# Order of loads, stores and the last division around the turned tile in a fused transformer layer

## The chip, the cores and the metric

The kernel runs on one core of a Trainium2 chip. The metric is the device time of one execution in microseconds, as the median of several runs. A profile of one execution was taken by the hardware profiler. The core's engines are TensorE (PE, with its weight loads as PEld), VectorE (DVE), ScalarE (ACT), GpSimd (POOL) and SyncE (SP, here the queue that issues most DMAs); each runs its instructions in the order of the program and waits for the others by semaphores.

## The reference

The input x has the shape (2, 256, 128, 128): batch, time T, bands FB, channels C. All is float32. Three residual steps follow one another:

```python
xt = _ln(x, ln_t_w, ln_t_b).transpose(0, 2, 1, 3)
x = x + _mha(xt, t_wi, t_bi, t_wo, t_bo, H_T, cm).transpose(0, 2, 1, 3)   # over time, causal
xf = _ln(x, ln_f_w, ln_f_b)
x = x + _mha(xf, f_wi, f_bi, f_wo, f_bo, H_F, bm)                          # over bands, |i - j| <= 16
xn = _ln(x, ln_n_w, ln_n_b)
h = jax.nn.gelu(xn @ w1.T + b1, approximate=False)                         # 128 -> 512
x = x + (h @ w2.T + b2)                                                    # 512 -> 128
```

Both attentions have 4 heads of 32 channels.

## The kernel before

The work is cut into 384 groups of 512 tokens, each kept as 128 partitions by 4 tiles by 128 channels. The first 128 groups are attention over time (class `OverTime`); they write their result to DRAM. Then come 16 runs of 16 groups: eight groups of attention over bands (`OverBands`) and, on the same tokens, eight groups of the feed-forward layer (`FeedForward`). A run of groups is called a run below, its band groups B0 to B7 and its feed-forward groups F0 to F7.

Every group passes the same stations. `load` brings x from DRAM (for band groups one DMA of 256 KB, `x<-x` in the profile). `statistics` and `root` make mean and variance (`stats`, `mv`, VectorE) and the inverse root (`rstd`, GpSimd). `normalize` makes `xh` and `turn` a transposed tile `z`, both on VectorE; `turn` also issues four DMAs from z to a DRAM tile `turned`. `fetch` issues one DMA that brings the turned tile back as `xnT`, channels on partitions, which is what TensorE needs. A band group then makes queries and keys (`bank<-xnT,wf`), values, scores (`qT,kT`), exponentials `pf`, their sums (`pf,ones`) and weighted values (`pf,v`); `divide` divides by the sums on VectorE and yields `oT`; `output` multiplies by the output weights (`wn,oT`); `finish` adds the residual on VectorE (`x<-bank,x`). A feed-forward group makes the hidden layer (`bank<-xnT,w1f`, 16 products for every one of its two halves), the gelu on ScalarE (`hT`), the second product (`w2T_sb,hT`) and the residual (`res`); `put` stores pairs of groups to `out`.

One loop over n, in `run`, issues pieces of about 18 groups at a time: it loads group n + 14, fetches n + 2, turns n + 3 (and in parts of a run n + 6), does the main products of n, and divides, outputs and finishes n - 1 and n - 2. The order in which the loop's body calls the pieces is the order of the instructions on each engine. `bands[i]` and `feeds[i]` tell whether group n - 2 + i is a band or a feed-forward group; `turn` is true in the one step per run where n is F0 and n - 1 is B7, so that the division in it is the last one of the run. That last division is exact (`invert_exactly`: RECIPROCAL to `ln`, then `u` and `oT`); the others start from ScalarE's logarithm and exponential (`r`).

In the profile all of these instructions have line 979, that of a helper that passes every instruction on, so that they are told apart by their tiles.

Of the kernel before, what the change touches and what calls it, by code (L numbers as in the profile page):

```python
# [691 lines left out]
class OverTime(Attention):  # L692
# [5 lines left out]
    early, late = (1, 2), (0, 3)  # L698
# [285 lines left out]
class BoundedPath:  # L984
# [364 lines left out]
    def run(self, x, out):  # L1349
        groups = list(self.groups(x, out))  # L1350

        def do(n, *names):
            if 0 <= n < len(groups):
                for name in names:
                    getattr(groups[n], name)()

        def at(n, kind):
            return 0 <= n < len(groups) and isinstance(groups[n], kind)

        def do_at(n, kind, *names):  # L1360
            if at(n, kind):
                do(n, *names)
# [13 lines left out]
        def at_turn(i):  # L1376
            return not 0 <= i < len(groups) or hasattr(groups[i], "turned")

        def turn_ahead(n):
            for i in (n + 3, n + 6):  # L1380
                ahead = at(n + 3, OverBands) and at(i, OverBands) and i not in run0
                if not at(i, OverTime) and (i == n + 3 or ahead) and not at_turn(i):
                    do(i, "normalize", "turn")
# [8 lines left out]
        for n in range(len(groups) + 2):  # L1392
            feeds = [at(n - 2 + i, FeedForward) for i in range(5)]
            bands = [at(n - 2 + i, OverBands) for i in range(5)]
            turn = feeds[2] and bands[1]
# [61 lines left out]
            do_at(n + 2, (OverBands, FeedForward), "fetch")  # L1457

            self.storing = self.scalar if feeds[2] and n < len(groups) - NT else self.sync
            do_at(n - 2, FeedForward, "put")  # L1460
            if n == 3:
                k.late_rows()
            if n == 5:
                k.late_weights()
            for i in {0: (), 1: (), 2: (14, 15), 3: (16, 17)}.get(n, (n + 14,)):
                do(i, "load")
            turn_ahead(n)
            if n != 1:
                do_at(n + 4, OverTime, "normalize", "turn")
            if old is not None:  # L1470
                do(n - 2, "finish")
            if n == 0:
# [28 lines left out]
            if bands[1] and bands[2]:  # L1501
                groups[n - 1].keep = True
                groups[n - 2].keep_output = bands[3]
                groups[n - 1].divide(partial(do, n - 2, "finish"))
            else:
                do(n - 1, "divide")
            if n == 1:
                do(5, "normalize", "turn")
            if n == 2:
# [111 lines left out]
```

## Time and profile before

| | |
|---|---|
| median of 3 runs | 2633.51 us (2633.33 to 2635.23) |
| profiled execution: its own time, its span | 2635.07 us, 2633.3 us |
| TensorE, products busy | 2617.5 us (99%) |
| TensorE, weight loads busy | 1779.1 us (68%) |
| VectorE busy | 2136.7 us (81%) |
| GpSimd busy | 1960.3 us (74%) |
| ScalarE busy | 1820.1 us (69%) |
| granted TensorE clock | full speed over the whole span |
| DMA | 344.99 MB, mean 131 GB/s |

The span is the time from the first to the last instruction of the program; the execution's own time has the start and the end around it as well. Busy shares are averages over the first part (time, about 920 us) and the 16 runs. Products on TensorE overlap one another, and their ends are modelled, so what they wait is seen in the distances between their starts.

### The profile page before, as it was taken

The page shows a single profiled execution, that of the slowest core. Times are in us where ns is not written, and L with a number is a line of the kernel's source. Part 1 is how long each engine was busy: PE and PEld are TensorE (multiplying, and loading weights), DVE is VectorE, ACT ScalarE, POOL GpSimd, SP SyncE. Part 2 cuts the span into 40 slices and gives each one's busy share as a digit, 9 for nine tenths or more (in the row PEclk, how much of TensorE's full clock was granted, in tenths as well). Part 3 has the DMA queues.
Part 4 walks back from the last instruction along what each step waited for, and adds up shares of the span by engine and source line. Part 5 has one row for each costly group of instructions (what it writes and reads, how often), then busy time and mean ns, then how long its engine had stood idle before and what let it go on. Part 6 is the DMA issues. An engine that isn't in the chain of part 4 may idle for free.

```text
span 2633.3 us, 156638 instructions
## 1 busy us (share of the span) xinstructions
PE 2617.5 (99%) x68688; PEld 1779.1 (68%) x68688; DVE 2136.7 (81%) x6410; ACT 1820.1 (69%) x3543; POOL 1960.3 (74%) x2311
## 2 busy tenths in 40 slices
PE   9999999999999999999999999999999999999999
PEld 6666676667666666667666666666666676666665
DVE  8888888888888888878779788787787887977874
ACT  7889999998998875564655745646557466475563
POOL 7999999999999977766666666666676666657762
PEclk9999999999999999999999999999999999999999
DMA  6656556566565455445454454554544544545443
GB/s 156 164 148 158 148 152 155 150 154 156 144 156 150 122 131 139 105 117 131 106 142 116 117 133 107 131 131 107 142 109 118 133 110 124 132 105 141 106 102 88
DMA packets 469798, 344.99 MB, mean 131 GB/s; under 512 B 43120, under 2 KB 404464, under 8 KB 469104
## 3 DMA queue, kind: packets, MB, share of 16 engines
q1 hardware_dynamic: 418360, 310.28, 47.4%
q10 hardware_dynamic: 50744, 24.59, 3.4%
q8 instruction: 541, 8.86, 1.5%
q14 instruction: 153, 1.25, 0.2%
HBM read 167.98 MB, written 166.72 MB: 127 GB/s over the span
## 4 chain that ended last, share of the span: by engine, by line
PE 87%; DVE 9%; issue 1%; DMA 1%; POOL 1%; ACTq 0%; SPq 0%; ACT 0%; DVEq 0%; POOLq 0%
PE bank L979 87%; DVE xh L979 2%; DVE bank L979 1%; DVE ln L979 1%; DVE stats L979 1%; DVE u L979 1%; DVE x L979 1%; DVE oT L979 1%; POOL rstd L979 1%; DVE z L979 0%; DMA xnT<-turned 0%; DVE mv L979 0%; ACTq L979 0%; DMA turned<-z 0%; SPq L979 0%
## 5 line engine op out<-in xcount | busy, mean ns | idle before, releaser
L979 ACT ACTIVATE hT<-bank,b 128x512 f32<-128x512 f32 x512 | 342.1, 688 | 534.4 <-PE bank L979 368.8
L979 POOL TENSOR_SCALAR_AFFINE_SELECT pf<-pf 128x512 f32<-128x512 f32 x768 | 478.3, 637 | 244.0 <-ACT pf L979 217.6
L979 PEld LDWEIGHTS bank<-w2T_sb,hT 128*32 128x32 f32 x16384 | 466.2, 110 | 137.1 <-issue 109.2
L979 PE MATMUL bank<-xnT,wf 128*32 128x512 f32 x4096 | 511.5, 593 | 1.0 <-DVE xnT L979 0.5
L979 PE MATMUL bank<-w2T_sb,hT 128*32 128x128 f32 x16384 | 498.2, 273 | 0.8 <-issue 0.5
L979 PE MATMUL bank<-xnT,w1f 128*32 128x512 f32 x4096 | 497.9, 592 | 0.0
L979 ACT ACTIVATE p<-bank 128x512 f32<-128x512 f32 (+1 forms) x1024 | 430.7, 494 | 63.2 <-PE bank L979 62.9
L979 DVE TENSOR_SCALAR xh<-x,mv,rstd 128x160 f32<-128x160 f32 (+1 forms) x1012 | 392.4, 430 | 59.8 <-POOL rstd L979 49.4
L979 POOL TENSOR_SCALAR_AFFINE_SELECT p<-p 128x1024 f32<-128x1024 f32 (+2 forms) x384 | 365.0, 951 | 55.4 <-ACT p L979 47.1
L979 PEld LDWEIGHTS bank<-wf,xnT 128*32 128x32 f32 x8192 | 237.0, 110 | 151.5 <-issue 89.8
L979 POOL TENSOR_TENSOR p<-p,p 128x512 f32<-128x512 f32 x256 | 324.6, 1291 | 10.7
L979 DVE BATCH_NORM_STATS2 stats<-x 128x6 f32<-128x128 f32 x1536 | 328.9, 276 | 3.3 <-DMA x<-in_x 3.3
L979 DVE TENSOR_TENSOR bank<-bank,r 128x512 f32<-128x512 f32 x240 | 166.2, 693 | 194.0 <-ACT r L979 116.1
L979 PE MATMUL bank<-qT,kT 32*64 32x80 f32 (+4 forms) x16384 | 303.7, 271 | 3.0 <-issue 2.9
L979 PEld LDWEIGHTS bank<-qT,kT 32*64 32x64 f32 x16384 | 260.9, 131 | 55.0 <-ACT kT L979 50.7
L979 ACT ACTIVATE pf<-bank 128x512 f32<-128x512 f32 x512 | 264.4, 602 | 37.6 <-PE bank L979 37.5
L979 POOL TENSOR_SCALAR rstd<-mv 128x4 f32<-128x4 f32 x251 | 57.7, 230 | 304.8 <-DVE mv L979 304.1
L979 DVE STREAM_TRANSPOSE z<-xh 128x512 f32<-128x512 f32 x380 | 270.4, 711 | 15.2 <-DMA turned<-z 1.8
L979 PE MATMUL bank<-wn,oT 128*32 128x128 f32 x8192 | 278.3, 274 | 1.1 <-DVE oT L979 0.3
L979 POOL TENSOR_TENSOR rstd<-rstd,mhalf 128x4 f32<-128x4 f32 x251 | 260.8, 1039 | 20.9
L979 PE MATMUL bank<-wf,xnT 128*32 128x128 f32 x8192 | 272.8, 273 | 0.0
L979 PEld LDWEIGHTS bank<-wn,oT 128*32 128x32 f32 x8192 | 221.2, 110 | 25.6 <-DVE oT L979 12.6
(100 smaller groups left out, 3713.3 us busy)
## 6 DMA issues: line engine op xcount, KB each, us to landing
turned<-z SPq DMA_DIRECT2D x1520, 64.0 KB, 2.6
xnT<-turned SPq DMA_DIRECT2D x380, 256.0 KB, 3.4
x<-res SPq DMA_DIRECT2D x256, 128.0 KB, 2.5
x<-x SPq DMA_DIRECT2D x128, 256.0 KB, 4.6
x<-in_x SPq DMA_DIRECT2D x124, 256.0 KB, 4.4
out<-res ACTq DMA_DIRECT2D x184, 128.0 KB, 3.0
out<-res SPq DMA_DIRECT2D x68, 128.0 KB, 3.5
x<-in_x SPq DMA_DIRECT2D x4, 128.0 KB, 3.1
```

The costliest lines, as they stand in the source:

```text
L979: return self.tc.keep_in_program_order(emit(*args, **kwargs))
```

## The change

In a step that handles a band or feed-forward group (`ahead`), the load of group n + 14 is issued after `turn_ahead`, that is after the four DMAs of the turned tile; before, it was issued ahead of them. In the steps where n is a band group, the store of group n - 2 (`put`) is issued there too. In the one step of a run where `turn` is true, `turn_ahead` and what follows it now come after the division of B7; before, they came ahead of it. `turn_ahead` itself is unchanged.

```diff
             self.storing = self.scalar if feeds[2] and n < len(groups) - NT else self.sync
-            do_at(n - 2, FeedForward, "put")
+            if not bands[2]:
+                do_at(n - 2, FeedForward, "put")
...
-            for i in {0: (), 1: (), 2: (14, 15), 3: (16, 17)}.get(n, (n + 14,)):
-                do(i, "load")
-            turn_ahead(n)
+            def late(n=n, bands=bands):
+                if bands[2]:
+                    do_at(n - 2, FeedForward, "put")
+                do(n + 14, "load")
+
+            ahead = at(n, (OverBands, FeedForward))
+            if not ahead:
+                for i in {0: (), 1: (), 2: (14, 15), 3: (16, 17)}.get(n, (n + 14,)):
+                    do(i, "load")
+            if not turn:
+                turn_ahead(n)
             if n != 1:
                 do_at(n + 4, OverTime, "normalize", "turn")
+            if ahead and not turn:
+                late()
...
                 do(n - 1, "divide")
+            if turn:
+                turn_ahead(n)
+                late()
             if n == 1:
```

What this does to the order shows on two engines. On VectorE, at the end of the second run, before: `ln`, `u` and `oT` are the division of B7, `xh` and `z` belong to F3, the TENSOR_TENSOR on x is the `finish` of B6, and the last rows are the statistics of F4.

```order
L979 BN_STATS stats<-x_20822 128x6 x4
L979 BN_AGGR mv<-stats 128x2 x4
L979 TENSOR_SCALAR xh<-x_20822,mv,rstd 128x5x32 x4
L979 STREAM_TRANSPOSE z<-xh 128x512
L979 RECIPROCAL ln<-bank_112 128x512
L979 TENSOR_TENSOR x_21409<-bank_110,x_21409 128x512
L979 TENSOR_TENSOR u<-bank_114,ln 128x4x4x32
L979 TENSOR_SCALAR oT<-u 128x512
L979 BN_STATS stats<-x_21409 128x6 x4
```

And the same place after the change:

```order
L979 BN_STATS stats<-x_20834 128x6 x4
L979 BN_AGGR mv<-stats 128x2 x4
L979 RECIPROCAL ln<-bank_112 128x512
L979 TENSOR_TENSOR x_21421<-bank_110,x_21421 128x512
L979 TENSOR_TENSOR u<-bank_114,ln 128x4x4x32
L979 TENSOR_SCALAR oT<-u 128x512
L979 TENSOR_SCALAR xh<-x_20834,mv,rstd 128x5x32 x4
L979 STREAM_TRANSPOSE z<-xh 128x512
L979 BN_STATS stats<-x_21421 128x6 x4
```

The division and the residual addition within it have moved ahead of the normalization and the transposition of F3; this happens at all 16 ends of runs and is the only move on VectorE.

On SyncE, at the start of the second run, before (`out` is the store of the run before, `x` the load of a group of a later run):

```order
L979 DMA turned_22748<-z_22746 32x4x128 x4
L979 DMA xnT_22892<-turned_22301 128x512
L979 DMA out<-res_22249 32x8x128 x4
L979 DMA turned_22905<-z_22903 32x4x128 x4
L979 DMA xnT_23013<-turned_22438 128x512
L979 DMA x_23015<-x1_0_94 32x16x128
L979 DMA xnT_23138<-turned_22569 128x512
L979 DMA x_23015<-x1_0_94 32x16x128
L979 DMA xnT_23274<-turned_22748 128x512
L979 DMA x_23015<-x1_0_94 32x16x128
L979 DMA xnT_23410<-turned_22905 128x512
L979 DMA x_23015<-x1_0_94 32x16x128
```

And after, the same place and the rows that follow:

```order
L979 DMA turned_22901<-z_22899 32x4x128 x4
L979 DMA out<-res_22249 32x8x128 x4
L979 DMA xnT_23013<-turned_22438 128x512
L979 DMA x_23015<-x1_0_94 32x16x128
L979 DMA xnT_23138<-turned_22569 128x512
L979 DMA x_23015<-x1_0_94 32x16x128
L979 DMA xnT_23274<-turned_22748 128x512
L979 DMA x_23015<-x1_0_94 32x16x128
L979 DMA xnT_23410<-turned_22901 128x512
L979 DMA turned_23419<-z_23417 32x4x128 x4
L979 DMA x_23015<-x1_0_94 32x16x128
L979 DMA xnT_23558<-turned_23419 128x512
```

The stores (four DMAs, 15 times in the program) have gone behind the four turned DMAs, and so has each load that shares a step with a turned tile (78 loads), which puts the load between the turned DMAs and the fetch of that same turned tile. A load in a step without a turned tile stays where it was. TensorE, ScalarE and GpSimd keep their order.

## The prediction

> **What bounds the kernel now.** I read the page first: busy shares, then the chain that ended last (the queue's row has packets, MB and share of the DMA engines).
>
> ```profile
> span 2633.3 us, 156638 instructions
> PE 2617.5 (99%) x68688; PEld 1779.1 (68%) x68688; DVE 2136.7 (81%) x6410; ACT 1820.1 (69%) x3543; POOL 1960.3 (74%) x2311
> ...
> q8 instruction: 541, 8.86, 1.5%
> ...
> PE 87%; DVE 9%; issue 1%; DMA 1%; POOL 1%; ACTq 0%; SPq 0%; ACT 0%; DVEq 0%; POOLq 0%
> ```
>
> TensorE (PE) is busy for 99% of the span and carries 87% of the chain; the change takes no product away. So all that can be won is time in which PE's products start later than their steady pace. That is not read from busy time, since products overlap and their ends are modelled; it is read from starts. Next come the waits of PE and of its weight loads (PEld): engine, tile, releaser, then total us, times, longest.
>
> ```profile
> PEld bank L979 <- ACT hT L979: 21.6, 67, 0.4
> ...
> PEld bank L979 <- DVE oT L979: 12.9, 15, 1.1
> ...
> PE bank L979 <- issue: 5.4, 12, 1.3
> ```
>
> Two rows matter here: oT, the divided attention output that VectorE (DVE) makes, waited for 15 times, about once per run (there are 16); and "issue", where nothing that the program shows was waited for. The 12.9 us are idle time of the weight loads, which run ahead of the products, so they are a ceiling and not the loss. The loss I take from the timeline around the end of a run (start us, duration us, engine; the run whose last division starts at 1086.36):
>
> ```profile
> 1081.57 1.04 PE L979 MATMUL bank<-pf,ones 128*32 128x512 f32 x8
> 1082.24 0.36 DVE L979 BATCH_NORM_AGGREGATE mv<-stats 128x2 f32<-128x6 f32 x4
> 1084.08 1.61 DVE L979 TENSOR_SCALAR xh<-x,mv,rstd 128x160 f32<-128x160 f32 x4 [1.48 <-POOL rstd L979]
> 1084.17 1.90 PE L979 MATMUL bank<-xnT,w1f 128*32 128x512 f32 x16
> 1085.72 0.71 DVE L979 STREAM_TRANSPOSE z<-xh 128x512 f32<-128x512 f32 x1
> 1086.36 3.32 DVE L979 RECIPROCAL ln<-bank 128x512 f32<-128x512 f32 x1
> 1089.60 0.63 DVE L979 TENSOR_TENSOR x<-bank,x 128x512 f32<-128x512 f32 x1
> 1090.15 0.68 DVE L979 TENSOR_TENSOR u<-bank,ln 128x512 f32<-128x512 f32 x1
> 1090.24 1.04 PE L979 MATMUL bank<-xnT,w1f 128*32 128x512 f32 x8
> 1090.86 0.43 DVE L979 TENSOR_SCALAR oT<-u 128x512 f32<-128x512 f32 x1
> 1091.20 0.86 DVE L979 BATCH_NORM_STATS2 stats<-x 128x6 f32<-128x128 f32 x4
> 1091.34 1.08 PE L979 MATMUL bank<-wn,oT 128*32 128x128 f32 x32
> 1092.24 1.90 PE L979 MATMUL bank<-xnT,w1f 128*32 128x512 f32 x16
> ```
>
> VectorE idles 1.48 us for rstd, then normalizes (xh) and turns (z) a later group, and only then starts the division (RECIPROCAL, then u, then oT). The sums that the division needs were done at 1081.57 + 1.04 = 1082.61. PE's output product starts at 1091.34, the moment oT is there (1090.86 + 0.43 = 1091.29).
>
> **The change part by part.**
>
> *The last division of a run goes ahead of the normalization.* From the first hidden product of the run's second feed-forward group to that of its third, PE takes 1092.24 - 1084.17 = 8.07 us here. One run later PE arrives late for another reason, oT is already there, and the same stretch shows the pace without the wait:
>
> ```profile
> 1192.35 0.66 PE L979 MATMUL bank<-xnT,w1f 128*32 128x512 f32 x3
> ...
> 1200.15 0.66 PE L979 MATMUL bank<-xnT,w1f 128*32 128x512 f32 x3
> ```
>
> That is 7.80 us: the wait costs 0.27 us. I took this stretch for all 16 runs from PE's rows: two have 7.80 (this one and the twelfth), the others 8.02 to 8.18, so 0.22 to 0.38 each, 4.07 us over 14 runs. After the change the division starts when the sums are done: 1082.65 at the latest of its inputs. From RECIPROCAL to the end of oT takes 1091.29 - 1086.36 = 4.93 us, so oT ends at 1087.58, some 3.5 us before PE comes for it at 1091.07. All of the wait goes: -4.1 us. Bounds: 0 if something else is late at that place, -12.9 if all idle time of the weight loads counted; I take 4.1, since it is measured on PE's own starts.
>
> *What becomes late instead.* xh and z come behind oT. They take 1086.43 - 1084.08 = 2.35 us, so z ends at 1089.93 and not at 1086.43: 3.5 us later, at the 15 or 16 ends alike. z goes to DRAM (turned, four DMAs) and comes back as xnT; both are issued on SyncE's queue (SPq):
>
> ```profile
> 1085.27 0.44 SPq L979 DMA_DIRECT2D x<-x  x1
> 1086.46 1.75 SPq L979 DMA_DIRECT2D turned<-z  x4
> 1091.56 0.34 SPq L979 DMA_DIRECT2D xnT<-turned  x1
> 1091.93 0.43 SPq L979 DMA_DIRECT2D x<-x  x1
> ...
> 1098.31 1.90 PE L979 MATMUL bank<-xnT,w1f 128*32 128x512 f32 x16
> ...
> 2576.19 3.09 SPq L979 DMA_DIRECT2D turned<-z  x4
> 2580.65 0.34 SPq L979 DMA_DIRECT2D xnT<-turned  x1
> ...
> turned<-z SPq DMA_DIRECT2D x1520, 64.0 KB, 2.6
> xnT<-turned SPq DMA_DIRECT2D x380, 256.0 KB, 3.4
> ...
> x<-x SPq DMA_DIRECT2D x128, 256.0 KB, 4.6
> ```
>
> (The last three are issues: KB each, median us from issue to landing.) PE wants this xnT with the second eight of the 16 products at 1098.31, one step of 0.86 us later: 1099.17, and 0.27 earlier after the change, 1098.90. New path: z at 1089.93, four issues 1.75, then the wait for turned to land, then issue and landing of xnT, 3.4. The wait for turned is 1091.56 - 1088.21 = 3.35 us in this run and 2580.65 - 2579.28 = 1.37 in the last. With 1.37 xnT lands at 1096.5, 2.4 us early; with 3.35 at 1098.4, 0.5 early. So no wait at PE by the median landing; I count 0, and keep as its bound 1.6 us a run from the rival below. The statistics behind it start at 1089.93 and not at 1091.20, since the 1.48 us of waiting for rstd are now filled with division: the next group's z gains 1.3 us.
>
> *Loads issued behind the turned tile.* 78 loads x<-x, each 0.44 us of SPq, change places with a group's four turned DMAs. turned starts up to 0.5 us earlier and no longer has 256 KB just ahead of it; x comes up to 1.8 us plus the wait for z later. No product waits for either: x is loaded 14 groups ahead and first read by the residual's bias addition 8 groups ahead, six steps of some 7 us later (1099.17 - 1092.24 = 6.93 is one). Gain and loss on PE: 0. SPq itself waits for z more often with the load queued behind it, but what stands behind the load is the next xnT, which needs the same turned tile anyway. If that cover of some 40 us were gone, a load would cost its 4.6.
>
> *The last stores of a run behind the turned tile.* 15 times four stores out<-res, on SPq. What is fetched next there was turned several groups before, and stands behind both either way; the res buffer is written again a whole run later. 0.
>
> PE's order and its waits are otherwise the same instruction for instruction, so the sum is -4.1 us. Against the profiled execution: span 2633.3 - 4.1 = 2629.2, and with the 1.7 us that lie around its span (its own time is 2635.07) 2631.0. That execution stands 1.6 us above the median of the runs, 2633.51; against the median the sum is 2629.4.
>
> **The rivals.** A measurement of this kernel tells 0.2% (5.3 us) from no change, so faster begins below 2628.2 and slower above 2638.8.
>
> *Slower: the fetch of xnT queues behind the moved load.* The load used to be ahead of turned and is now between turned and the fetch of what was turned. If its 256 KB go ahead of xnT as a whole, xnT lands later by about what a load takes over a turned DMA, 4.6 - 2.6 = 2.0 us (my estimate from these medians). The margin of 0.5 to 2.4 us above then becomes a wait of up to 1.5 us; at 15 ends, 15 x 1.5 - 4.1 = +18 us, 2651.9 at worst, and with half of that per end +7.2 us, 2640.7, which is the value I give it. It decides from (5.3 + 4.1) / 15 = 0.63 us per end on. The Trainium skill, "DMA: Bandwidth & Descriptors", section on queues, rings and completion order, says that each DMA engine takes the descriptors of a ring in the order of the ring; by it the load's bytes do precede xnT's, and the sum would be this rival's. Against it: a load 0.4 us behind the fetch, as at 1091.93 in this run, already shares the engines with xnT in the median of 3.4 us, and the fetch is issued at least 1.4 us after the load, by when much of the load is under way. Chance 0.07.
>
> *Faster: PE's instruction pages come sooner as well.* The 12 waits named "issue" are in mid-product-group, like this one:
>
> ```profile
> 2325.58 0.74 PE L979 MATMUL bank<-qT,kT 32*64 32x80 f32 x39
> 2326.10 0.44 SPq L979 DMA_DIRECT2D x<-x  x1
> 2327.58 0.51 PE L979 MATMUL bank<-qT,kT 32*64 32x80 f32 x25 [1.25 <-issue]
> ```
>
> The instruction queue moved 541 packets of 8.86 MB / 541 = 16.4 KB, and PE's 2 x 68688 instructions make 254 per packet. The eleven such stalls over 0.45 us that I followed in the bands' and feeds' part all fall on the same place modulo 256 instructions, and each ends 1.3 to 1.7 us after a packet has ended. So PE waits there for its own next page of instructions, and the page comes over the DMA engines that the moved loads use. If the new places of the loads let the pages through, up to 5.4 us more go: 2629.4 - 5.4 = 2624.0, half of that 2626.7, the value I give it. It decides from 1.2 us on. For it: some of these stalls lie just behind a load, as this one. Against: others lie beside turned or out DMAs, which stay, the bytes are the same, and pages may as well come later. The Trainium skill, "Runtime: NRT & Kernel Launch", instruction fetch mechanics, has pages of 16 KiB fetched while the current one runs, at a cost that is mostly hidden; the page size agrees with the 16.4 KB, and by "hidden" this rival would be worth nothing, where the row shows 5.4 us. Chance 0.26.
>
> *Nothing: the wait is refilled.* At the ends of runs PE then waits for ScalarE's hidden layer or the late xnT, 0.27 us a run: 2633.5. For it: the weight loads wait for the hidden layer's hT 67 times already. Against: 0.4 us is the longest of these, all of them within idle time that the weight loads have anyway, and in the two runs with 7.80 us nothing of the kind took the wait's place. Chance 0.07.
>
> **How the numbers follow.** The forecast, 4.1 us off and pages within 1.1 us of now: 0.60, 2629.4, with a range of its own of 2628.3 to 2630.5. Same is the forecast and the refilled wait, 0.67; faster 0.26; slower 0.07. The range goes from 2625.5, past the middle of the faster rival, to 2634.0, past the refilled wait; what lies outside is the slower rival and the rest of the faster, under 0.2.
>
> **What would show it.** In the changed profile: the PEld wait for oT falls from 15 times to one or two; RECIPROCAL follows the aggregated statistics without the 1.48 us of idle time, and oT ends some 3.5 us before its product; the stretch of 8.07 us is 7.80 in all runs; z at the ends is 3.5 us later and the fetch of xnT lands still ahead of its product. The forecast is wrong if that product shows PE waiting for xnT, or if the "issue" waits change by more than 1.2 us.

## The result, and the profile after

The changed kernel took 2637.91 us (median of 22 runs, 2632.70 to 2647.36) where the kernel before took 2633.42 (22 runs, 2629.96 to 2639.59) beside it: 1.0018 times as long, 95% interval 1.0010 to 1.0027. That is about 4.5 us slower, where 4.1 us faster was forecast, and 3.9 us above the range. The profiled execution took 2638.89 us, its span 3.5 us more than that of before.

The page of the changed kernel: the span, the busy shares, and the shares of the chain that ended last.

```profile
span 2636.8 us, 156624 instructions
PE 2617.1 (99%) x68688; PEld 1792.5 (68%) x68688; DVE 2139.3 (81%) x6410; ACT 1823.9 (69%) x3543; POOL 1960.2 (74%) x2311
...
PE 98%; DMA 1%; issue 0%; SPq 0%; DVE 0%; ACT 0%; ACTq 0%; DVEq 0%
```

TensorE is as busy as before, to 0.4 us, and the chain no longer runs over VectorE (9% before, 0% now). So what VectorE cost is gone, and the time has gone to something that neither the busy shares nor the chain show. The waits of the changed kernel (engine, tile, releaser, then total us, times, longest):

```profile
PEld bank L979 <- ACT pf L979: 11.4, 8, 2.1
...
PE bank L979 <- issue: 7.3, 10, 2.1
...
PE bank L979 <- DMA xnT<-turned: 2.3, 5, 0.8
```

The weight loads' wait for oT (12.9 us, 15 times) is down to 0.3 us, once. Instead "issue" has grown from 5.4 to 7.3 us in fewer and longer pieces. PE now waits five times for an xnT, which it did not before, and its weight loads wait eight times for pf, which the products that follow the scores read (before, 1.2 us in two pieces).

Where the time went shows in the starts of PE's products, step by step. I took the first product on xnT of each step of the bands (B0 to B7), subtracted the shortest distance to the next step from each of the 16 runs' distances, and summed. From B4 to B5 that sum is 2.1 us before and 11.7 after: before, 13 runs have the bare 6.23 us; after, ten runs have from 0.14 to 2.55 us more. The next worst is B5 to B6, 0.2 before and 1.7 after. B3 to B4 has 3.2 and 3.7, but of different kinds: before, three of its four longer runs have an "issue" wait there; after, in all six of them B4's first product starts 0.13 us behind the landing of its xnT, and the five waits for xnT stand at that product. The balance: -4.1 us at the ends of runs (below), +9.6 from B4 to B5, 5.5 together against 3.5 in the spans; the rest lies in small pieces of both signs that I didn't follow.

The worst of these stretches, on PE, in the changed kernel (start us, duration us, engine, operation):

```profile
2117.13 1.04 PE L979 MATMUL bank<-xnT,wf 128*32 128x512 f32 x8
...
2123.80 0.96 PE L979 MATMUL bank<-qT,kT 32*64 32x80 f32 x64 [2.14 <-issue]
...
2125.91 1.95 PE L979 MATMUL bank<-xnT,wf 128*32 128x512 f32 x8
```

From B4's first product to B5's it takes 2125.91 - 2117.13 = 8.78 us, and 2.14 of them are one "issue" wait in front of the scores. Its queue SPq just ahead, first of the kernel before:

```profile
2099.59 2.10 SPq L979 DMA_DIRECT2D out<-res  x4
2104.35 2.94 SPq L979 DMA_DIRECT2D turned<-z  x4
2107.39 0.39 SPq L979 DMA_DIRECT2D xnT<-turned  x1
2107.88 0.39 SPq L979 DMA_DIRECT2D x<-x  x1
2108.36 0.44 SPq L979 DMA_DIRECT2D xnT<-turned  x1
2108.85 0.42 SPq L979 DMA_DIRECT2D x<-x  x1
2111.93 0.34 SPq L979 DMA_DIRECT2D xnT<-turned  x1
```

And of the changed kernel, the same place in the program:

```profile
2107.91 2.84 SPq L979 DMA_DIRECT2D turned<-z  x4
2110.79 2.00 SPq L979 DMA_DIRECT2D out<-res  x4
2112.89 0.43 SPq L979 DMA_DIRECT2D xnT<-turned  x1
2113.42 0.98 SPq L979 DMA_DIRECT2D x<-x  x1
2114.49 0.44 SPq L979 DMA_DIRECT2D xnT<-turned  x1
2114.98 0.42 SPq L979 DMA_DIRECT2D x<-x  x1
2115.50 0.44 SPq L979 DMA_DIRECT2D xnT<-turned  x1
```

This is where the loss begins. Before, the stores went out while the queue had nothing else to do: from 2101.69 to 2104.35 it waited for z. Behind the turned tile they stand in front of the fetch of B4's xnT. That fetch is issued 4.24 us ahead of its product (2117.13 - 2112.89) where it was 7.00 ahead before (B4 starts at 2114.39 there); over the 15 runs that have these stores the mean is 4.45 against 7.39. What follows also closes up. Before, two pairs of fetch and load went out, and the third 3 us later. After, the three fetches go out within 3.1 us (2112.89 to 2115.94) and each has a load behind it (the third at 2115.99), 1.5 MB in all. What the DMA engines then do, in 3 us windows, the two ahead of B4's first product and the two behind it, before (window, length, busy time of PE, PEld, DVE, ACT and POOL, clock, DMA share, GB/s):

```profile
2108.39:2111.39 3.00, 3.00 (x96) 2.40 (x92) 1.56 (x3) 2.28 (x5) 2.66 (x5) 1.00 0.92 232
2111.39:2114.39 3.00, 2.49 (x93) 1.44 (x85) 1.66 (x3) 1.65 (x4) 0.14 (x1) 1.00 0.94 239
2114.39:2117.39 3.00, 3.00 (x80) 2.13 (x76) 0.62 (x2) 2.96 (x6) 2.86 (x5) 1.00 0.28 64
2117.39:2120.39 3.00, 3.00 (x112) 2.01 (x108) 2.42 (x5) 1.72 (x4) 0.73 (x2) 1.00 0.07 16
```

And after:

```profile
2111.13:2114.13 3.00, 3.00 (x80) 2.14 (x76) 0.74 (x2) 2.77 (x6) 2.79 (x6) 1.00 0.79 201
2114.13:2117.13 3.00, 3.00 (x108) 1.88 (x104) 2.46 (x4) 1.94 (x4) 0.71 (x2) 1.00 0.89 237
2117.13:2120.13 3.00, 3.00 (x80) 2.14 (x76) 0.59 (x2) 2.97 (x6) 2.86 (x5) 1.00 1.11 217
2120.13:2123.13 3.00, 1.52 (x40) 0.92 (x32) 2.06 (x4) 1.20 (x3) 0.78 (x2) 1.00 0.55 91
```

The DMA engines are nearly full for six microseconds before (0.92, 0.94, then 0.28), and for nine after, into B4 (0.79, 0.89, 1.11; more than one since packets overlap). And there PE runs out of instructions. Counted along PE's queue, with products, weight loads and semaphore waits together, every "issue" wait of both kernels stands at the same place modulo 256 (193 or 194); I take it for the boundary between two pages of instructions, and the packets of the instruction queue (541 of 16.4 KB, as the prediction has them) for the pages. In this run the packet of the page that PE then waits for starts 5.08 us after PE has crossed the boundary ahead of it; the mean from B4 to B5 is 1.86 us after the change and 1.18 before, whose latest is 2.26. PE goes on 1.44 us after the packet's end. The same holds for the other steps: in all ten longer ones from B4 to B5 PE falls behind at such a boundary, with 10.7 of the 11.7 us between the third product ahead of it and the twelfth behind it.

### The profile page after: what moved, and what is told of

Read it like the earlier page. It is cut to its first block, busy times and chain, and to the rows that moved or that the text cites. A ratio compares the mean times of both kernels' runs of the same rounds, so it can differ in the third digit from the quotient of the medians.

```text
span 2636.8 us, 156624 instructions
## 1 busy us (share of the span) xinstructions
PE 2617.1 (99%) x68688; PEld 1792.5 (68%) x68688; DVE 2139.3 (81%) x6410; ACT 1823.9 (69%) x3543; POOL 1960.2 (74%) x2311
## 3 DMA queue, kind: packets, MB, share of 16 engines
q8 instruction: 541, 8.86, 1.5%
## 4 chain that ended last, share of the span: by engine, by line
PE 98%; DMA 1%; issue 0%; SPq 0%; DVE 0%; ACT 0%; ACTq 0%; DVEq 0%
PE bank L979 98%; DMA xnT<-turned 1%; SPq L979 0%; DVE xh L979 0%; DMA x<-in_x 0%; ACT pf L979 0%; DVE z L979 0%; DVE bank L979 0%; DVE stats L979 0%; DVE xnT L979 0%; ACT v L979 0%; ACTq L979 0%; ACT p L979 0%; DVE vy L979 0%; ACT lnv L979 0%
## 5 line engine op out<-in xcount | busy, mean ns | idle before, releaser
L979 PEld LDWEIGHTS bank<-w2T_sb,hT 128*32 128x32 f32 x16384 | 475.2, 110 | 127.7 <-issue 103.3
L979 PE MATMUL bank<-w2T_sb,hT 128*32 128x128 f32 x16384 | 504.7, 273 | 0.4 <-issue 0.4
L979 PE MATMUL bank<-xnT,w1f 128*32 128x512 f32 x4096 | 504.8, 592 | 0.0
L979 POOL TENSOR_TENSOR p<-p,p 128x512 f32<-128x512 f32 x256 | 323.9, 1286 | 10.7
L979 DVE TENSOR_TENSOR res<-bank,res 128x512 f32<-128x512 f32 (+1 forms) x259 | 170.9, 660 | 93.1 <-PE bank L979 79.5
```

Of the source, the lines that this page charges most:

```text
L979: return self.tc.keep_in_program_order(emit(*args, **kwargs))
```

## The experiments

Each kernel was compared with the kernel before on the same chip; since chips differ (before took from 2629.5 to 2631.5 us there), the ratios count, and the last column gives the mean distance from the issue of B4's fetch to its product over the 15 later runs. "B4 to B5" is the sum over the runs beyond 6.23 us, "F1 to F2" the stretch of the prediction that was 8.02 to 8.18 us in 14 runs; both come from the one profiled execution of each kernel. Most of these lie near their kernel's median; that of e6 took 5.4 us more, and those of e7, e8 and e11 are the shortest of theirs, 3.2, 10.1 and 10.8 us under the median.

| kernel | ratio to before, 95% | B4 to B5, us | F1 to F2, us | PE on "issue", us | fetch ahead, us |
|---|---|---|---|---|---|
| before | 1 | 2.1 | 8.02 to 8.18 | 5.4 | 7.39 |
| after | 1.0018 (1.0010 to 1.0027) | 11.7 | 7.80 | 7.3 | 4.45 |
| e1, stores put back | 0.9980 (0.9971 to 0.9989) | 2.1 | 7.80 | 1.5 | 7.27 |
| e2, division alone | 0.9988 (0.9979 to 0.9996) | 2.9 | 7.80 | 1.4 | 7.15 |
| e3, stores alone | 1.0039 (1.0026 to 1.0052) | 10.8 | 8.01 to 8.2 | 7.1 | 4.29 |
| e4, loads alone | 1.0005 (0.9996 to 1.0014) | 1.4 | 7.91 to 8.19 | 2.4 | 7.20 |
| e5, stores behind the fetch | 0.9988 (0.9979 to 0.9997) | 4.0 | 7.80 | 2.4 | 7.13 |
| e6, small stores | 1.0017 (1.0008 to 1.0026) | 16.5 | 7.80 | 11.3 | 4.39 |
| e7, loads three steps later | 1.0051 (1.0037 to 1.0065) | 0.1 | 7.80 | 1.2 | 4.16 |
| e8, the same, stores put back | 1.0067 (1.0054 to 1.0081) | 0 | 7.80 | 0.9 | 7.06 |
| e9, loads out of the burst | 0.9976 (0.9967 to 0.9985) | 0.2 | 7.80 | 0.3 | 4.11 |
| e10, the same, stores put back | 0.9975 (0.9966 to 0.9984) | 0 | 7.80 to 7.83 | 0.4 | 7.27 |
| e11, e1 with the fetch held | 1.0067 (1.0047 to 1.0087) | 9.2 | 7.80 | 5.4 | 3.55 |

### The parts apart: e1 to e4

e1 puts the 15 stores back ahead of the turned tile and leaves the rest of the change. e2 has the division alone, e3 the stores alone, e4 the loads alone. Their edits are of the same kind; e1's, against the changed kernel, is this:

```diff
-            if not bands[2]:
-                do_at(n - 2, FeedForward, "put")
+            do_at(n - 2, FeedForward, "put")
...
             def late(n=n, bands=bands):
-                if bands[2]:
-                    do_at(n - 2, FeedForward, "put")
                 do(n + 14, "load")
```

> The changed kernel with the 15 stores of F7 put back ahead of the turned tile; division ahead and loads behind as changed. Theory S (the moved stores hold SyncE's queue while the fetch of B4 waits behind them, and crowd the DMA engines): the loss goes and the division's 4.1 us stay, 4 us below the kernel before, step B4 to B5 at 6.23 us in nearly all runs. Rival L (the moved loads crowd them): as the changed kernel, 4 to 5 us above the kernel before, with B4 to B5 steps of 7 us and more.

> Only the last division of a run goes ahead of normalization; loads and stores stand as before the change. Both theories: 4.1 us below the kernel before, every step F1 to F2 at 7.80 us. If instead the later z of F3 makes the fetch late, F3's first product waits and the gain is under 2 us.

> Only the 15 stores of F7 go behind the turned tile. Theory S: 8 to 9 us above the kernel before (the changed kernel's 4.5 and the 4.1 that its division saves), the fetch of B4 some 3 us later, B4 to B5 steps longer by 0.6 us a run on average. Rival L: within 1 us of the kernel before.

> Only the 78 loads go behind the turned tile. Theory S: within 1 us of the kernel before. Rival L: 8 to 9 us above it, with the longer steps where loads are, B2 to F1.

The whole loss is the stores. Without them the change is 0.20% faster (e1), with them alone 0.39% slower (e3), and the step from B4 to B5 follows them: 2.1 and 2.9 us without, 10.8 and 11.7 with. The loads alone are nothing that can be told from no change. The product of the three parts, 0.9988 x 1.0039 x 1.0005 = 1.0032, lies above the whole, 1.0018 (up to 1.0027); the intervals of the parts are as wide as that difference, and whether the parts help one another stays open. In e3 the weight loads' wait for oT is there as before, beside the larger one on "issue":

```profile
PEld bank L979 <- DVE oT L979: 15.1, 17, 1.1
PE bank L979 <- issue: 7.1, 10, 1.7
```

In e1 it is the other way round: one wait of 0.3 us for oT, and 1.5 us on "issue" in two pieces. That e1, e2 and e4 have less of "issue" than before (1.4 to 2.4 us against 5.4) is not explained; single stalls come and go with small shifts of time, and each figure is from one execution.

### What of the stores it is: their bytes, their place, or the loads behind them (e5 to e8)

e5 issues the stores one step later, behind the fetch of B4's xnT. e6 leaves them in the changed place and lets each carry 16 KB and not 128 (seven eighths of these rows of `out` are not written). e7 lets all loads of the late kind be made for group n + 11 and not n + 14, which takes them from the steps around B4; e8 is e7 with the stores put back.

```diff
e5, in late:
-                if bands[2]:
-                    do_at(n - 2, FeedForward, "put")
   and ahead of it, behind the fetch:
+            elif at(n - 2, OverBands):
+                do_at(n - 3, FeedForward, "put")
e6, in store:
+                        part = 1 if g == NT - 1 and t0 % RUN == GB else n * NT
...  both sides of the DMA:
+                                [:, 0:part]
e7, in late:
-                do(n + 14, "load")
+                do(n + 11, "load")
```

> The changed kernel with the stores of F7 one place further back: behind the fetch of B4, ahead of the load of that step. The fetch is not held any more, but the same 512 KB go out at the same time as two more fetches and three loads. Theory crowding (the store's bytes keep TensorE's instruction pages waiting on the DMA engines): the loss stays, 3 to 5 us above the kernel before, steps B4 to B5 over 6.23 us by 8 to 12 us in sum. Rival holding (the fetch of B4 and all behind it are issued 3 us later): the loss goes, 4 to 5 us below the kernel before, sum under 3 us.

> The changed kernel, where each of the four stores of F7 writes one of its eight rows per partition, 16 KB and not 128 KB; seven eighths of these rows of out are left out. Their place in the queue and their number stay. Crowding: 4 to 5 us below the kernel before, sum of the B4 to B5 excess under 3 us, although the fetch of B4 still comes some 2 us later than with the stores in the old place. Holding: the fetch is still about 2 of 3 us late, so 1 to 3 us above the kernel before.

> The changed kernel with every load of these steps three steps later (group n + 11 and not n + 14), so that no load stands between the fetches of B4, B5 and B6; stores as changed. Crowding: 768 KB less beside the stores, so most of the loss goes, 2 to 5 us below the kernel before. Holding: the fetch of B4 is held by the stores as in the changed kernel, 4 to 5 us above the kernel before.

> The kernel with the stores put back and the division ahead, and the loads three steps later as well; meant as a version that beats both. Crowding: as good as the stores put back or better, 5 to 7 us below the kernel before, since what is left of the waits for instruction pages stands in the bands' first steps. Holding: 5 us below, no more. Either is wrong if the loads now crowd steps F2 to F4 or come too late for their statistics: then it is slower than with the stores put back.

e6 takes most of the stores' bytes away, and nothing gets better: 1.0017, and B4 to B5 loses 16.5 us. So it isn't what the stores carry. SPq and PE in one run of e6:

```profile
1472.39 2.98 SPq L979 DMA_DIRECT2D out<-res  x4
1475.47 0.37 SPq L979 DMA_DIRECT2D xnT<-turned  x1
...
1484.47 0.88 PE L979 MATMUL bank<-qT,kT 32*64 32x80 f32 x54
1487.13 0.49 PE L979 MATMUL bank<-qT,kT 32*64 32x80 f32 x10 [1.78 <-issue]
```

The issue of four small stores takes nearly as long as that of the large ones (median over the 15 moved groups 2.91 us here, 3.17 in the changed kernel; 2.03 before, in the old place), and the fetch stands behind them all the same. e5 has the same stores in full and only the order with the fetch exchanged. SPq in one of its runs:

```profile
1042.66 1.76 SPq L979 DMA_DIRECT2D turned<-z  x4
1044.53 0.39 SPq L979 DMA_DIRECT2D xnT<-turned  x1
1044.96 1.99 SPq L979 DMA_DIRECT2D out<-res  x4
```

Its ratio is 0.9988, with 4.0 us from B4 to B5, a little short of what holding was expected to give back (under 3 us). So it is the place ahead of the fetch, for most of the loss.

e7 and e8 bring B4 to B5 to within 0.03 us of its bare 6.23 us in every run, so without the loads in the burst the stores cost nothing there. As kernels both miss: they are slower than before by 0.51% and 0.67%. The loss has moved to the step from B0 to B1, which lost 17.9 us in e7 and 17.3 in e8 beyond its shortest distance, and PE waits there for kT from ScalarE. The waits of e7:

```profile
PE bank L979 <- ACT kT L979: 11.6, 9, 2.4
```

The group of ScalarE that makes the hidden layer, in the list of groups of e7 (count, busy, mean ns, idle time before, and what ended it):

```profile
L979 ACT ACTIVATE hT<-bank,b 128x512 f32<-128x512 f32 x512 | 343.4, 688 | 547.4 <-PE bank L979 401.4 <-DMA out<-res 126.9 <-DVE z L979 5.1
```

The loads now lie in the steps in which ScalarE issues the stores, and of its idle time there 126.9 us are put down to a store, against 80.4 before. I didn't follow that further; it shows that loads have bad places of their own in this kernel.

### Holding the fetch without stores, and the stores without the burst (e9 to e11)

e9 is the changed kernel with the loads of the steps of B2, B3 and B4 made two a step in B5 to B7 instead; e10 is e9 with the stores put back. e11 is e1 with six loads of 16 bytes on each of 32 partitions, into a tile that nothing reads, ahead of the fetch of B4's xnT: a hold with hardly a byte.

```diff
e9, in late:
-                do(n + 14, "load")
+                p = (n - run0[0]) % (2 * A)
+                for i in {2: (), 3: (), 4: (), 5: (11, 12), 6: (12, 13), 7: (13, 14)}.get(p, (14,)):
+                    do(n + i, "load")
e11, ahead of the fetch:
+            if at(n, OverBands) and at(n - 3, FeedForward) and bands[0]:
+                for i in range(6):
+                    self.sync.dma_start(self.held[...], ...[:, 0:1, 0:4])
```

> The changed kernel, stores as changed; the three loads of steps B2 to B4 are made in B5 to B7, two a step, so that the fetches of B4, B5 and B6 follow one another without loads. Theory hold-and-burst (the stores hold the fetch of B4, and the burst of three fetches and three loads behind it, 1.5 MB, then falls into step B4 and keeps PE's instruction pages waiting): the B4 to B5 excess goes to under 2 us, 3 to 5 us below the kernel before. Rival hold alone (the late fetch itself is the cost): the excess stays at 8 us or more, 4 us above the kernel before.

> The same with the stores put back; meant as a version that beats both. Hold-and-burst: 4 to 7 us below the kernel before; no burst and no hold. It is slower than with the stores put back alone if two loads a step crowd B5 to B7.

> The kernel with the stores put back, and six tiny loads (16 bytes to each of 32 partitions, into a tile that nobody reads) ahead of the fetch of B4, which hold the queue for 2.6 us or more without bytes. If holding the queue there is the cause, with or without the loads' bytes, the loss comes back: B4 to B5 excess of 8 us or more, 2 to 6 us above the kernel before. If it takes the stores themselves, as with the stores put back, 5 us below.

SPq in one run of e11:

```profile
1043.52 2.17 SPq L979 DMA_DIRECT2D turned<-z  x4
1045.73 3.61 SPq L979 DMA_DIRECT2D held<-in_x  x6
1049.44 0.38 SPq L979 DMA_DIRECT2D xnT<-turned  x1
```

With the stores in their old place, 3.61 us of queue time ahead of the fetch bring the loss back: 9.2 us from B4 to B5 in its profiled execution, where e1 has 2.1, and 5.4 us on "issue", where e1 has 1.5. The whole of e11 is 0.67% slower than before (16 us by the medians), more than the 2 to 6 us that were expected. Its six executions go from 2634.8 to 2659.8 us, and the profiled one is the shortest of them; what the longer ones lost beyond it is not shown.

e9 has the stores in the changed place, and its fetch is as late as in the changed kernel (4.11 us ahead). SPq at that place (the last row merges the fetches of B4 to B7, the first issued at 2100.75):

```profile
2096.11 2.51 SPq L979 DMA_DIRECT2D turned<-z  x4
2098.66 1.99 SPq L979 DMA_DIRECT2D out<-res  x4
2100.75 9.49 SPq L979 DMA_DIRECT2D xnT<-turned  x4
```

From B4's first product, at 2105.34, to B5's it takes the bare 6.23 us. The windows on both sides of it, as above:

```profile
2102.34:2105.34 3.00, 3.00 (x108) 1.88 (x104) 2.46 (x4) 1.94 (x4) 0.70 (x2) 1.00 0.76 201
2105.34:2108.34 3.00, 3.00 (x80) 2.14 (x76) 0.59 (x2) 2.97 (x6) 2.86 (x5) 1.00 0.15 57
```

And PE's wait on "issue" in the whole of e9:

```profile
PE bank L979 <- issue: 0.3, 1, 0.3
```

Where the DMA share behind B4's start is 0.15 and not 1.11, the late fetch cost nothing. So it takes both: something that holds the queue, and a burst behind it that the hold pushes into B4. e9 and e10 have the lowest ratios here, 0.24% and 0.25% below before (their intervals overlap that of e1), and between them the place of the stores no longer matters.

## Why the prediction was wrong

**The step that failed** is the last of the change's parts: "The last stores of a run behind the turned tile", "0". Measured alone it is +0.39% (0.26 to 0.52), about +10 us. Its reason, "What is fetched next there was turned several groups before, and stands behind both either way", is true of the order and false of the time. Before, the four stores took 2.10 us in the run shown, in which SPq would have waited for z anyway; behind the turned tile their 2 to 3 us come after that wait, and the fetch is 3 us nearer to its product. I had priced the stores by who reads what they touch, and not by whether the queue had been idle where they stood. The timeline of SPq before has that gap, and I hadn't looked there.

**The division** was right in size and way. In the changed kernel, at the end of the run that the prediction quoted:

```profile
1083.94 3.36 DVE L979 RECIPROCAL ln<-bank 128x512 f32<-128x512 f32 x1
...
1088.47 0.43 DVE L979 TENSOR_SCALAR oT<-u 128x512 f32<-128x512 f32 x1
1088.81 1.60 DVE L979 TENSOR_SCALAR xh<-x,mv,rstd 128x160 f32<-128x160 f32 x4
1090.45 0.71 DVE L979 STREAM_TRANSPOSE z<-xh 128x512 f32<-128x512 f32 x1
```

PE, in the same stretch:

```profile
1085.43 1.90 PE L979 MATMUL bank<-xnT,w1f 128*32 128x512 f32 x16
...
1092.36 1.06 PE L979 MATMUL bank<-wn,oT 128*32 128x128 f32 x32
1093.23 1.90 PE L979 MATMUL bank<-xnT,w1f 128*32 128x512 f32 x16
```

oT ends at 1088.90, 3.46 us ahead of its product at 1092.36 (3.5 forecast), and the stretch is 1093.23 - 1085.43 = 7.80 us, as in all 16 runs. That is the -4.1 us of the prediction on PE's starts; the division alone made the kernel 0.12% (0.04 to 0.21) faster, 3.2 us of 2630.

**z and its fetch** were right: xnT of F3 lands ahead of its product in every run, by 1.1 us at least in the changed kernel. The margin is as thin as forecast: in e9 and e11 one of these fetches comes late, by 0.7 and 0.5 us. **The loads** were right: 0 forecast, 1.0005 (0.9996 to 1.0014) measured.

**The rivals.** "Slower: the fetch of xnT queues behind the moved load" has the wrong culprit; with the loads alone nothing of it showed. The rule that it took from the Trainium skill, "DMA: Bandwidth & Descriptors", queues, rings and completion order, is that descriptors are taken in the order of their ring, by which the load's go ahead of xnT's. e4 has that order in its queue, and nothing of the price showed. Its kind, something new ahead of a fetch on SPq, was the cause all the same, at another fetch. "Faster: PE's instruction pages come sooner as well" had the right resource and the wrong sign: the text named it against itself, "pages may as well come later", and gave that case no chance of its own. Its bound was right too, as e9 shows: with the burst out of the way, the waits on "issue" go from 5.4 to 0.3 us. "Nothing: the wait is refilled" didn't happen at the ends of runs. The last line of the prediction holds: "issue" changed by 1.9 us, over the 1.2 that it set. None of the cases was this one: the pages later, at +9.6 us from B4 to B5.

**What is shown and what isn't.** Shown by runs: the stores' place ahead of the fetch is the cause (e1, e3, e5), their bytes aren't (e6), a hold with hardly a byte does it as well (e11), and only with loads in the burst behind it (e7, e9). That the loss is late instruction pages is read from the traces: PE falls behind at one place modulo 256 of its queue, and the pages are late where the DMA share is high. The pages themselves were not moved in any run. The five waits for xnT, 2.3 us, are the late fetch itself; they stand in the step from B3 to B4, in the place of the "issue" waits that it had before. Why pages suffer in B4 and less in B3, which is as crowded in the kernel before (0.94) and lost 3.2 us there, is open.

## What to carry to other kernels

Before moving a DMA on a queue, look at whether the queue is idle where the DMA stands now: here an issue in a wait for a semaphore was free, and the same issue behind that wait delayed every fetch after it. When a late fetch can be borne, ask what goes out with it, since a delayed queue catches up in a burst, and a burst can take time from transfers that no line of the program shows, as the instruction pages are. Read the distances between equal steps of the bound engine, run by run: at a busy share of 99% before and after they found the 9.6 us.

## What was not expected of the hardware

The instruction pages of TensorE are a real cost beside bursts: 5.4 us of waits before, 7.3 after, 11.3 with small stores, 0.3 with the loads spread, at the same bytes (541 packets, 8.86 MB, in all of them). The Trainium skill, "Runtime: NRT & Kernel Launch", instruction fetch mechanics, has pages fetched ahead at a cost that is mostly hidden; the trace of e9 (0.3 us) agrees, and that of e6 (11.3 us) does not. And a DMA's issue time here hardly followed its bytes: four stores of 16 KB held the queue for 2.91 us, four of 128 KB for 3.17 (medians), and six loads of 0.5 KB for 3.61 in the run shown.
